# Expert blocks of a decoder layer: gate and up computed with features on partitions, from weights copied by VectorE, with grouped loads and later sums

## The chip, the cores and the metric

The kernel runs on one core of a Trainium2 chip. The metric is the device time of one execution in microseconds (us), less is better; for several executions the median is given. One execution was also taken by the hardware profiler. The profile's engines are TensorE (PE for matmuls, PEld for its weight loads), VectorE (DVE), ScalarE (ACT), GpSimd (POOL) and SyncE (SP); a q behind a name is that engine's sequencer, which handles waits, registers and the issue of DMAs.

## The reference

One decoder layer in fp32 on x of 16 sequences x 256 tokens x 256 features: attention with rope and a Taylor softmax, an additive cross term, and a mixture of experts. Only the last part is touched:

```python
shared = silu(x @ ws_gate) * (x @ ws_up) @ ws_down
scores = sigmoid(x @ gate_w.T)                       # 16 experts
topk_w, topk_idx = top_k(scores, 2)
topk_w = topk_w / (topk_w.sum(-1) + 1e-20) * 2.5
g = einsum('th,ehm->etm', x, w_gate)                 # h 256, m 128
u = einsum('th,ehm->etm', x, w_up)
eo = einsum('etm,emh->eth', silu(g) * u, w_down)
out = einsum('te,eth->th', route, eo) + shared
```

The reference computes all experts for all tokens; the kernel computes for each token only its two chosen ones.

## The kernel before

**First stage.** Attention and the cross term run sequence by sequence, in an order written out by hand (ORDER, DRAIN). At its end each token is normalised, its two experts are chosen, and the row (256 features, the two weights, the expert's code and the destination, 264 numbers in all) is scattered twice by GpSimd's indirect DMA into the DRAM tensor `listed`, in which each expert owns whole blocks of 128 rows. The weights of all experts lie in SBUF: `wgu_sb` for gate and up, `wd_sb` for down.

**Block stage.** There are NB = 79 blocks at most; the last five are run only if they are needed, under a branch (`unusual_blocks`), and were not needed here. The other USUAL = 74 run in a loop of steps (lines 1180 to 1206) whose instruction order on each engine is the order of the code, since the loop is under a manual schedule. A block i passes through:

- load, nine steps ahead (AHEAD): one DMA on SP of 128 rows, line 272, into one of 14 buffers `rows`; the first six go to room in `h3T`, from `begin_blocks`.
- `turn`, step i: two TensorE transposes (line 283) put features on partitions, ScalarE copies them to `rowsT` (line 286).
- `pick`, step i: three VectorE operations on one number per row (lines 293, 296, 300) find the weight of the row and its destination.
- `hidden_product`, step i+2: `gu` with tokens on partitions, the rows stationary and the expert's weights moving (line 308, an address from a register that `expert_of` loads for four blocks at a time, line 350). ScalarE takes Silu of the gate half (line 314).
- `weigh`, step i+2: VectorE multiplies Silu, the row's weight and the up half (line 318).
- `turn_hidden`, step i+3: a TensorE transpose `th` (line 325), VectorE copies it to `hidT` (line 327).
- `give`, step i+4: down (line 331), ScalarE copies it out of PSUM to `got` (line 337), GpSimd scatters the rows to `given` in DRAM (line 338), at the destination.

An fp32 matmul is issued as two MATMUL instructions, each with a weight load of its own, a transpose as one. So a step has four MATMULs of line 308, one of 325, two of 331 and two of 283.

**Sums.** When all blocks that can hold rows of a sequence have been given, SP fetches the two results of its 256 tokens (`fetch`, line 1100), at the step in `due`: three steps (LANDED) after the last give, near the end one. VectorE adds them to `x_all` in four adds of 128x256 (line 1120), one a step, the first FETCHED = 6 steps after the fetch; then SP stores the sequence (line 1114). What is left over at the end of the loop is added in the tail (`tail_adds`), between the shared experts of the last four sequences (`SharedLate`, lines 1134 to 1149), which fill TensorE while the last scatters land.

**Queues and buffers.** SP issues block loads, fetches and stores in program order and waits in that order. VectorE, ScalarE and GpSimd run their instructions in program order. PSUM has two buffers each for `tp`, `gu`, `th` and `eo`. The pools of the block stage reuse memory of the first stage, so that the first instructions there wait for many semaphores.

Of the kernel before, what the change touches and what calls it, by code (L numbers as in the profile page):

```python
# [44 lines left out]
F32 = mybir.dt.float32  # L45
# [31 lines left out]
def decoder_kernel(  # L77
# [188 lines left out]
    codes = None  # L266

    class Block:
        def __init__(self, i, home, rows=None, rowsT=None):
            self.i, self.home, self.rowsT = i, home, rowsT  # L270
            self.rows = self.tile("rows", [P, ROW]) if rows is None else rows
            ins = nc.sync.dma_start(out=self.rows, in_=listed[ts(i, P)])
            behind(ins, enlisted)
            enlisted.clear()
# [13 lines left out]
        def pick(self):  # L288

            code, own = self.rows[:, D + 2 : D + 3], codes[:, self.i : self.i + 1]  # L290
            self.weight = self.tile("weight", [P, 1])
            self.dest = self.tile("dest", [P, 1], I32)
            nc.vector.scalar_tensor_tensor(
                self.weight, code, own, self.rows[:, D : D + 1], ALU.is_equal, ALU.mult
            )
            nc.vector.scalar_tensor_tensor(
                self.dest, code, own, self.rows[:, D + 3 : D + 4], ALU.is_equal, ALU.add
            )

            nc.vector.tensor_tensor(  # L300
                self.weight, self.weight, self.rows[:, D + 1 : D + 2], ALU.max
            )

        def hidden_product(self, e):
            self.e = e
            gu = self.gu = self.tile("gu", [P, 2 * M])
            for k in range(KT):
                nc.tensor.matmul(  # L308
                    gu, lhsT=self.rowsT[:, k],
                    rhs=wgu_sb[:, ds(e, 1), k].rearrange("p a i m -> p (a i m)"),  # L310
                    start=(k == 0), stop=(k == KT - 1),
                )
            self.hid = self.tile("hid", [P, M])
            nc.scalar.activation(self.hid, gu[:, 0:M], AF.Silu)  # L314

        def weigh(self):

            nc.vector.scalar_tensor_tensor(  # L318
                self.hid, self.hid, self.weight, self.gu[:, M : 2 * M],
                ALU.mult, ALU.mult,  # L320
            )
# [765 lines left out]
    with tc.tile_pool(name="ew", bufs=3) as ew, tc.tile_pool(  # L1087
# [92 lines left out]
        for i in range(max(due) + 1):  # L1180
# [4 lines left out]
            if 2 <= i < USUAL + 2:  # L1185
                blocks[i - 2].hidden_product(expert[i - 2])
# [68 lines left out]
```

## Time and profile before

| | us |
|---|---|
| median of five executions | 505.56 (504.3 to 509.84) |
| the profiled execution | 505.42 |
| its span, first to last instruction | 503.6 |
| TensorE busy | 471.6 |
| VectorE busy | 385.8 |
| ScalarE busy | 329.3 |
| GpSimd busy | 321.9 |
| granted TensorE clock, mean | 0.992 |
| block stage, from the first gate-up product to the end | 362.4 to 503.6 |

The span is cut into slices in the page, and for each engine the busy share is given in tenths. A table by windows gives for a stretch the busy time of PE, PEld, DVE, ACT and POOL with the number of their instructions, then the granted clock, the share of the DMA engines and the GB/s. In a timeline a line is start, duration, engine, source line, operation, out<-in, shape and count; merged instructions have the duration of their union. A bracket tells how long the engine stood idle before and what ended that. The duration of a MATMUL includes its drain, which overlaps the next one's stream, so that the cost of one in a sequence is the distance to the next start.

### The profile page before, as it was taken

Reading aid. Unit: us, or ns where it says so; the run is one execution under the profiler, and the core shown is the slowest. Engines: PE = TensorE matmul, PEld = TensorE weight load, DVE = VectorE, ACT = ScalarE, POOL = GpSimd, SP = SyncE. Lnnn points to the kernel's source line nnn. Section 1 sums busy time; section 2 is a strip of 40 time slices with the busy share of each in tenths; the row PEclk is TensorE's granted clock in tenths of the full one; section 3 lists DMA queues with packets and bytes.
Section 4 is the critical chain, followed back from the end, with each engine's and each line's share of the span. In section 5 each row is a group of like instructions: output and inputs, shape, how many; then the busy total and the mean of one; then the engine's idle time right before and its main releaser. Section 6 shows DMA issues by size and latency. Waiting matters only on the chain. (4 is left out here: it accounts for less than half of the span.)

```text
span 503.6 us, 12732 instructions
## 1 busy us (share of the span) xinstructions
PE 471.6 (94%) x4078; PEld 315.4 (63%) x4078; DVE 385.8 (77%) x1607; ACT 329.3 (65%) x783; POOL 321.9 (64%) x539
## 2 busy tenths in 40 slices
PE   2999999999999999999999999988799999999994
PEld 1455656656656656656656655545588888887882
DVE  5745557879989989989989877998555567766766
ACT  2378789887787887887887898331255555555530
POOL 5765346687888888888886666575155665555550
PEclk9999999999999999999999999998999999999998
DMA  7896551342333323321210211111565367987765
GB/s 206 253 342 214 172 171 33 96 131 75 117 77 125 117 73 131 117 79 61 65 44 25 56 33 55 44 54 54 145 211 167 100 203 237 299 286 265 224 196 178
DMA packets 61139, 69.68 MB, mean 138 GB/s; under 512 B 7164, under 2 KB 52493, under 8 KB 61072
## 3 DMA queue, kind: packets, MB, share of 16 engines
q1 hardware_dynamic: 53760, 50.88, 34.0%
q0 software_dynamic: 6624, 17.05, 9.1%
q10 hardware_dynamic: 688, 0.92, 0.6%
q8 instruction: 34, 0.56, 0.5%
q14 instruction: 33, 0.27, 0.2%
HBM read 36.89 MB, written 33.24 MB: 139 GB/s over the span
## 5 line engine op out<-in xcount | busy, mean ns | idle before, releaser
L655 ACT ACTIVATE a<-sc 128x1024 f32<-128x1024 f32 x128 | 124.7, 1032 | 25.1 <-PE sc L645 24.3
L338 POOL DMA_INDIRECT given<-block_got,block_dest x74 | 72.7, 983 | 62.3 <-ACT block_rowsT L286 42.0
L901 POOL DMA_INDIRECT listed<-h,slots x64 | 66.9, 1046 | 16.3 <-issue 15.8
L645 PE MATMUL sc<-qT,kT 32*128 32x256 f32 x1024 | 75.7, 401 | 0.9 <-ACT a L655 0.9
L308 PE MATMUL block_gu<-wgu_sb,block_rowsT 128*128 x288 | 74.4, 381 | 0.1
L645 PEld LDWEIGHTS sc<-qT,kT 32*128 32x128 f32 x1024 | 47.5, 184 | 31.1 <-ACT kT L589 9.1
L665 PE MATMUL av<-a,vaug 128*32 128x256 f32 x1024 | 65.8, 381 | 0.1
L549 PE MATMUL pq<-wqkv,hT 128*128 128x512 f32 x128 | 64.4, 629 | 0.7 <-ACT hT L539 0.7
L327 DVE COPY block_hidT<-block_th 128x128 f32<-128x128 f32 x74 | 21.6, 292 | 40.9 <-PE block_th L325 27.9
L571 POOL TENSOR_TENSOR qkr<-rot,m 128x512 f32<-128x512 f32 x32 | 41.0, 1285 | 17.6 <-DVE m L565 9.5
L308 PEld LDWEIGHTS block_gu<-wgu_sb,block_rowsT 128*128 128x128 f32 x288 | 49.2, 190 | 4.4 <-ACT block_hid L314 0.3
L381 POOL TENSOR_TENSOR rs<-rs,neg_half 128x2 f32<-128x2 f32 x64 | 48.1, 752 | 5.3
L314 ACT ACTIVATE block_hid<-block_gu 128x128 f32<-128x128 f32 x74 | 20.6, 278 | 35.9 <-PE block_gu L308 12.9
L331 PE MATMUL block_eo<-wd_sb,block_hidT 128*128 x148 | 44.1, 381 | 0.0
L665 PEld LDWEIGHTS av<-a,vaug 128*32 128x32 f32 x1024 | 29.3, 110 | 21.2 <-issue 6.3
L387 POOL TENSOR_SCALAR h<-x_all,neg,rs 128x256 f32<-128x256 f32 x64 | 40.1, 632 | 3.4
L337 ACT COPY block_got<-block_eo 128x256 f32<-128x256 f32 x74 | 27.6, 373 | 20.2 <-issue 14.9
L676 ACT ACTIVATE xs<-av,vsum 128x256 f32<-128x256 f32 x64 | 27.3, 485 | 16.4 <-PE av L665 16.4
L559 DVE TENSOR_TENSOR rot<-pq,cosf 128x512 f32<-128x512 f32 x32 | 22.0, 686 | 17.9 <-PE pq L549 17.8
L549 PEld LDWEIGHTS pq<-wqkv,hT 128*128 128x128 f32 x128 | 23.0, 199 | 19.6 <-issue 17.3
L597 PE MATMUL pv<-wqkv,hT 128*128 128x256 f32 x128 | 30.4, 380 | 0.2 <-DVE m L565 0.2
L711 PE MATMUL py<-wo_sb,wvT 128*128 128x256 f32 x128 | 30.4, 380 | 0.0
(190 smaller groups left out, 978.6 us busy)
## 6 DMA issues: line engine op xcount, KB each, us to landing
listed<-empty SPq DMA_DIRECT2D x9, 1056.0 KB
block_rows<-listed SPq DMA_DIRECT2D x68, 132.0 KB
sum<-given SPq DMA_DIRECT2D x15, 512.0 KB
x_all<-in_x_dram SPq DMA_DIRECT2D x16, 256.0 KB
c<-in_ctx_dram SPq DMA_DIRECT2D x16, 256.0 KB
out_dram<-x_all SPq DMA_DIRECT2D x15, 256.0 KB
enc_row<-enc_rows SPq DMA_DIRECT2D x16, 128.0 KB
wgu_sb<-in_L_ffn_w_gate_dram SPq DMA_DIRECT2D x16, 128.0 KB
```

What stands on the lines that cost most here:

```text
L308: nc.tensor.matmul(gu, lhsT=self.rowsT[:, k], rhs=wgu_sb[:, ds(e, 1), k].rearrange("p a i m -> p (a i m)"), start=(k == 0), stop=(k == KT ...
L331: nc.tensor.matmul(eo, lhsT=self.hidT, rhs=wd_sb[:, ds(self.e, 1)].rearrange("m a d -> m (a d)"), start=True, stop=True,)
L338: ins = nc.gpsimd.indirect_dma_start(out=given, out_offset=bass.IndirectOffsetOnAxis(ap=self.dest, axis=0), in_=got, in_offset=None, bound ...
L381: nc.gpsimd.tensor_tensor(r, r, neg_half, ALU.pow)
L387: nc.gpsimd.tensor_scalar(h[:, t, 0:D], src[:, t], neg[:, t : t + 1], r[:, t : t + 1], ALU.add, ALU.mult)
L549: nc.tensor.matmul(pq.rearrange("p h i two -> p (h i two)"), lhsT=self.hT[:, k, ts(t, P)], rhs=wqkv[:, k, 0 : 2 * D], start=(k == 0), stop ...
L571: nc.gpsimd.tensor_tensor(self.qkr[:, t], self.rot[t].rearrange("p h d -> p (h d)"), self.m2[t].rearrange("p h i two -> p (h i two)"), ALU ...
L597: nc.tensor.matmul(self.pv[:, t], lhsT=self.hT[:, k, ts(t, P)], rhs=wqkv[:, k, 2 * D : 3 * D], start=(k == 0), stop=(k == KT - 1),)
L645: nc.tensor.matmul(scs[j // 2][:, j % 2, kt], lhsT=self.kT[rows, g % 2, g // 2, ts(kt, P)], rhs=self.qT[rows, g // 2], start=True, stop=True,)
L655: nc.scalar.activation(a, self.scs[g][i], AF.Square, bias=1.0, scale=HD**-0.5)
L665: nc.tensor.matmul(self.av[ts(j, 32), g % 2], lhsT=self.va[:, kt, head], rhs=self.a[g, j // 2][:, j % 2, kt], start=(kt == 0), stop=(kt == ...
L901: ins = nc.gpsimd.indirect_dma_start(out=listed, out_offset=bass.IndirectOffsetOnAxis(ap=self.slots[:, i, t : t + 1], axis=0), in_=self.h3 ...
```

## The change

- `hidden_product` makes `gu` with features on partitions: the expert's weights are stationary and `rowsT` moves, gate and up for themselves, 128 columns each. The result needs no turn, so `turn_hidden` and its PSUM buffers are gone; `gu` and `eo` have three buffers each.
- The stationary weights come from a tile `w` (four buffers): `weights`, step i, is a VectorE copy of 128x512 from `wgu_sb` at an address from a register. VectorE therefore loads the expert's number too.
- The row's weight is no longer applied in the gating product (`gated`, two operands) but as a scale per partition in the copy of down's result from PSUM on ScalarE.
- A `Group` loads four blocks with one DMA from block 6 on, into one of five buffers, and picks for four blocks at once, in four VectorE operations of 128x4. The first six blocks have a group each, with loads and picks for themselves.
- `give` comes at step i+3, the fetches one step earlier with it, and FETCHED is 9 with five buffers `sum`.

The DMAs that load the blocks are now, in program order on SP, 17 of four blocks and the first six of one. Per block TensorE has eight MATMULs for gate and up in place of four, and two each for down and the turn of the rows as before. VectorE's order in a step is: the copy for block i, the gating of block i-2, in one step of four the picks, then an add. The first instruction of the stage on VectorE is the register load, then the copy for block 0.

```diff
+    class Group:
+        def __init__(self, i, n, home, rows=None):
...
+                self.rows = self.tile("rows", [P, n, ROW])
+            ins = nc.sync.dma_start(
+                out=self.rows, in_=listed[i * P : (i + n) * P].rearrange("(n p) d -> p n d", p=P)
+            )
...
+        def pick(self):
...
+            first, second, code, last = (self.rows[:, :, D + i] for i in range(4))
+            own = codes[:, self.i : self.i + self.n]
...
+            nc.vector.tensor_tensor(same, code, own, ALU.is_equal)
+            nc.vector.tensor_tensor(self.weight, same, first, ALU.mult)
+
+            nc.vector.tensor_tensor(self.weight, self.weight, second, ALU.max)
+            nc.vector.tensor_tensor(self.dest, same, last, ALU.add)
...
-        def hidden_product(self, e):
+        def weights(self, e):
             self.e = e
-            gu = self.gu = self.tile("gu", [P, 2 * M])
-            for k in range(KT):
-                nc.tensor.matmul(
-                    gu, lhsT=self.rowsT[:, k],
-                    rhs=wgu_sb[:, ds(e, 1), k].rearrange("p a i m -> p (a i m)"),
-                    start=(k == 0), stop=(k == KT - 1),
-                )
-            self.hid = self.tile("hid", [P, M])
-            nc.scalar.activation(self.hid, gu[:, 0:M], AF.Silu)
-
-        def weigh(self):
-            nc.vector.scalar_tensor_tensor(
-                self.hid, self.hid, self.weight, self.gu[:, M : 2 * M],
-                ALU.mult, ALU.mult,
-            )
-
-        def turn_hidden(self):
-            th = self.tile("th", [P, M])
-            nc.tensor.transpose(th, self.hid, ident)
-            self.hidT = self.tile("hidT", [M, P])
-            nc.vector.tensor_copy(self.hidT, th)
+            self.w = self.tile("w", [P, KT, 2, M])
+            nc.vector.tensor_copy(self.w.unsqueeze(1), wgu_sb[:, ds(e, 1)])
+
+        def hidden_product(self):
+            gu = self.gu = self.tile("gu", [M, 2, P])
+            for i in range(2):
+                for k in range(KT):
+                    nc.tensor.matmul(
+                        gu[:, i], lhsT=self.w[:, k, i], rhs=self.rowsT[:, k],
+                        start=(k == 0), stop=(k == KT - 1),
+                    )
+            self.hid = self.tile("hid", [M, P])
+            nc.scalar.activation(self.hid, gu[:, 0], AF.Silu)
+
+        def gated(self):
+            nc.vector.tensor_tensor(self.hid, self.hid, self.gu[:, 1], ALU.mult)
...
-                eo, lhsT=self.hidT,
+                eo, lhsT=self.hid,
...
-            nc.scalar.copy(got, eo)
+            nc.scalar.activation(got, eo, AF.Copy, scale=self.weight)
...
-            owner_row[:, i : i + n], engines=(mybir.EngineType.PE,), min_val=0, max_val=E - 1,
+            owner_row[:, i : i + n], min_val=0, max_val=E - 1,
+            engines=(mybir.EngineType.PE, mybir.EngineType.DVE),
...
-            got = ew.tile([P, TT, 2, D], F32, tag="sum", name="sum", bufs=4)
+            got = ew.tile([P, TT, 2, D], F32, tag="sum", name="sum", bufs=5)
...
-        AHEAD, LANDED, FETCHED = 9, 3, 6
+        AHEAD, LANDED, FETCHED = 9, 3, 9
...
-            step = last + 4 + (LANDED if last + 4 < USUAL - AHEAD else 1)
+            step = last + 3 + (LANDED if last + 3 < USUAL - AHEAD else 1)
...
+            if i < USUAL:
+                blocks[i].weights(expert[i])
             if 2 <= i < USUAL + 2:
-                blocks[i - 2].hidden_product(expert[i - 2])
-            if 3 <= i < USUAL + 3:
-                blocks[i - 3].turn_hidden()
+                blocks[i - 2].hidden_product()
             if i == USUAL + 2:
                 late[0].gate_up()
-            if 4 <= i < USUAL + 4:
-                blocks[i - 4].give()
+            if 3 <= i < USUAL + 3:
+                blocks[i - 3].give()
             if 2 <= i < USUAL:
                 blocks[i].turn()
             if 2 <= i < USUAL + 2:
-                blocks[i - 2].weigh()
+                blocks[i - 2].gated()
...
-            if i + AHEAD < USUAL:
-                blocks.append(Block(i + AHEAD, home))
+            load_blocks(i + AHEAD + 1)
```

## The prediction

> **What bounds the kernel now.** I read the page from the top: busy shares, slices, then the chain of waits, then the windows. TensorE is the bound almost throughout, and its granted clock is full.
>
> ```profile
> PE 471.6 (94%) x4078; PEld 315.4 (63%) x4078; DVE 385.8 (77%) x1607; ACT 329.3 (65%) x783; POOL 321.9 (64%) x539
> PE   2999999999999999999999999988799999999994
> PEclk9999999999999999999999999998999999999998
> ```
>
> The change touches only the block stage, about 362 us to the end. The table by windows shows that TensorE has no gap there in 84 us, VectorE is 64% busy and GpSimd 58%:
>
> ```profile
> 366.00:450.00 84.00, 84.00 (x467) 70.98 (x466) 53.61 (x283) 47.81 (x156) 48.96 (x50) 1.00 0.68 213
> ```
>
> So what a step costs is the sum of its matmul passes. The timeline of one step (start, duration; MATMULs overlap their drains, so I take distances between starts):
>
> ```profile
> 402.53 1.03 PE L308 MATMUL block_gu<-wgu_sb,block_rowsT 128*128 x4
> 403.39 0.27 PE L325 MATMUL block_th<-ident,block_hid 128*128 128x128 f32 x1
> 403.50 0.60 PE L331 MATMUL block_eo<-wd_sb,block_hidT 128*128 x2
> 403.94 0.38 PE L283 MATMUL block_tp<-ident,block_rows 128*128 128x128 f32 x2
> 404.16 1.03 PE L308 MATMUL block_gu<-wgu_sb,block_rowsT 128*128 x4
> ```
>
> Gate and up 0.86, turn of hid 0.11, down 0.44, two turns of rows 0.22: 1.63 us (exactly, 1.627: from 366 to 450 every step repeats to 0.01). 74 such steps are the stage.
>
> **Steady step.** Removed on TensorE: block_th, 0.11. Gate and up go from four passes of 256 columns (0.86) to eight of 128. No row has eight such passes in a run, but two come near: a pair of full 128-column fp32 passes, and passes of 32 columns whose pace can only be their weight load.
>
> ```profile
> 353.87 0.38 PE L1012 MATMUL po<-ident,total 128*128 128x128 f32 x2
> 344.77 0.38 PE L796 MATMUL ahead<-both,tri 128*128 128x32 f32 x2 [1.63 <-DVE norm L829]
> 344.99 0.39 PE L796 MATMUL ahead<-both,ones 128*128 128x32 f32 x2
> ```
>
> In the first, one pass takes 0.274 and two together 0.38, so the second starts 0.11 after the first. In the others two passes come each 0.22, so a weight load costs 0.11 too, though its record says 0.19: loads overlap. Eight passes: 8 x 0.110 = 0.88 (0.872 at 0.109, 0.896 at 0.112). The far bound, loads not overlapped at all, 8 x 0.19 = 1.52, is excluded by those rows. New step 0.88 + 0.434 + 0.218 = 1.532, against 1.627: -0.095 (-0.079 to -0.103). Over 70 steps, the first four being counted below: **-6.65** (-5.5 to -7.2).
>
> **What must hide beside it.** VectorE, by distances between starts in the same step: turn copy 0.20, weigh 0.26, three picks 0.33, an add 0.42: 1.21. The turn copy and the picks go (-0.53). Four picks of a whole group come once in four steps (dependent small operations follow each other in 0.21 on lines 877 to 881, so 0.6, 0.15 a step). That leaves 0.83. The weight copy, 128x512 from SBUF to SBUF, has no row. Above: the add of 512 columns at line 949, 0.605 from start to start (0.68 in the record). Below: half of its 0.53 of streaming, 0.34. VectorE is then 1.17 to 1.44 of 1.532: hidden by TensorE at either end, with little to spare at the upper one, so the sum does not turn on it; I take the middle, 0.47, which makes 1.30. A register load on VectorE each four steps (0.54 at line 1026) runs on its sequencer under the add.
>
> The Trainium skill, VectorE: DVE Perf Modes, section "The perf-mode tier table", gives an fp32 SBUF copy twice the rate (1227 ns for 2048), which as an estimate makes 0.42 us of ours and VectorE 1.25 a step, hidden, so the sum stays; no run here shows one. A rule against the change stands in the Trainium skill, SBUF — State Buffer, "Who interferes with whom": a copy in that mode and a GpSimd instruction hold one port pair and exclude each other for a whole instruction. By it VectorE could wait for a DMA_INDIRECT, and the sum would be about that of rival 2 in place of 499.3. The nearest row does not show that: a 16-column TENSOR_SCALAR on SBUF took 0.17 at 346.24, inside a DMA_INDIRECT from 346.19 to 347.17.
>
> ScalarE: the eviction got takes a scale per partition. COPY 0.373 now; a Copy with a scale at line 589 took 0.761 for 512 against 0.592 without, so +0.1 to +0.17: 0.28 + 0.37 + 0.5 = 1.15 a step, hidden. GpSimd: 0.98 a step, unchanged. Dependence: hid must be gated before down. TensorE has down, two turns and the next gate and up between (0.43 + 0.22 + 0.88 = 1.53); Silu 0.28, gating 0.34 and hand-overs take 0.8, so 0.7 is spare for a VectorE that runs late. Behind a late gating the next picks, add and weight copy queue; the copy is two steps early.
>
> Loads: SP issues 17 of 528 KB in place of 68 of 132 KB, same bytes, at least nine steps ahead (13.8 us), with 20 blocks of room against 14: 0. Should one be late, the turn of that block stops TensorE. Sums nine steps behind a fetch, three more than now: waits for them are 1.4 us in all, three times, most of it in the tail: 0 (-0.4). The output stores move back with the adds on SP, the fetches one step forward with give; both wait there for what they do now. A third PSUM buffer for gate-up and down takes the place of the turn's: 0, nothing waits for one now.
>
> **Start.** Here the copy is on the path: TensorE's first product needs it.
>
> ```profile
> 361.62 0.69 DVE L949 TENSOR_TENSOR x_all<-x_all,shared_eo 128x512 f32<-128x512 f32 x1 [0.70 <-PE shared_eo L942]
> 362.40 0.22 DVE L293 SCALAR_TENSOR_TENSOR block_weight<-h3T 128x1 f32<-128x1 f32 x1
> 362.41 1.10 PE L308 MATMUL block_gu<-wgu_sb,h3T 128*128 x4 [0.83 <-DVE x_all L949]
> ```
>
> VectorE's first block operation comes at 362.40 after its waits; now a register load (0.35 to 0.54) goes before them and the copy (0.34 to 0.69) must end: TensorE starts 0.9 to 1.3 later. Then VectorE has copy, four picks (0.6), copy, picks, copy before the first gating, some 2.4 to 3.2 after its start, while TensorE wants it 2.0 after its own: another 0.2 to 0.8. Together **+1.5** (+1.0 to +2.1).
>
> **Tail.** Give follows gating by one step instead of two, and the turn is gone.
>
> ```profile
> 482.40 1.03 PE L308 MATMUL block_gu<-wgu_sb,block_rowsT 128*128 x4
> 484.34 1.89 PE L1134 MATMUL late_ps<-h3T,wgu_sb 128*128 128x256 f32 x8
> 486.07 1.03 PE L331 MATMUL block_eo<-wd_sb,block_hidT 128*128 x4
> 488.62 0.98 POOL L338 DMA_INDIRECT given<-block_got,block_dest  x1 [0.30 <-issue]
> 496.56 3.27 DVE L1120 TENSOR_TENSOR x_all<-x_all,sum 128x256 f32<-128x256 f32 x8 [0.93 <-DMA sum<-given]
> 499.75 0.74 DVE L1149 TENSOR_TENSOR x_all<-x_all,late_eo 128x256 f32<-128x256 f32 x2
> ```
>
> Gate and up of the last block end at 483.26; its scatter starts 5.36 later. Now: down of block 72 0.43, late gate and up 1.73, down 0.43, eviction 0.7, 0.1: 3.4, a gain of 2.0 up to the fetch. But three more adds (3 x 0.39) are left for the tail. VectorE had 0.93 of idle before the last eight adds; it now reaches them about 12.3 after gate and up, with the fetch landed at 11.3, against 13.3 before. **-1.0** (-2.0 to +0.3).
>
> **Sum.** -6.65 + 1.5 - 1.0 = -6.15. The profiled execution took 505.42 (span 503.6 and 1.8 around it), 0.14 under the median of 505.56. 505.42 - 6.15 = **499.3**.
>
> **Rivals.** Let s be the step; the whole is 505.9 + 70 x (s - 1.627).
> 1. VectorE is just late: copy at 0.605, loads and waits of its sequencer not hidden (0.1 to 0.15), s = 1.59: **503.3**. For: picks add 0.45 in one step of four and the register load stands ahead of a copy. Against: 0.7 of slack.
> 2. Slower: the weight copy waits on VectorE for GpSimd. s = 0.83 + c, c the copy with its wait. No gain from c = 0.79; 1% slower (s above 1.695) from c = 0.87. A wait of half a DMA_INDIRECT, 0.49 on 0.47, gives s = 1.79: **517.3**. For: GpSimd is in one for 0.98 of each step. Against: the row at 346.24.
> 3. The change buys nothing because transfers set the pace: s stays 1.627, **505.9**. For: DMA slices at 9 tenths with 299 GB/s about 430. Against: no TensorE wait on rows anywhere from 366 to 450.
> 4. More gain: two pauses at 452 and 462, in which VectorE and ScalarE stood for up to 2.2 us, cost TensorE some 1.6 in all (window 450 to 483: 31.90 of 33.00 busy, and stretched ends). If late sums cause them, nine steps end them, and the tail gives its 2.0: **496.7**.
>
> **How the numbers follow.** Forecast 0.57 (its own range 497.5 to 501.5), rival 1 0.19, rival 2 0.13, rival 3 0.05, rival 4 0.06. Leaving out rival 2 and part of the edges, 496.5 to 506.0 holds about 0.8. A difference under 1% (500.5 to 510.6) is about what a measurement of this kernel cannot tell from none. Faster by more: 0.47 of the forecast's 0.57, all of rival 4 and little of rival 1, 0.55. Slower by more: 0.12 of rival 2. Rest 0.33.
>
> **What would show it.** Gate and up as eight passes 0.11 apart, TensorE full at a distance of 1.53 between blocks; the weight copy at 0.4 to 0.7, VectorE 80 to 90% busy; first product near 363.5; last adds without idle time before them. Wrong if passes come over 0.115 apart, if the copy or the DMA_INDIRECT stretches (rival 2), or if down waits for gating (rival 1).

## The result, and the profile after

| | before | after |
|---|---|---|
| median, us | 507.04 (504.18 to 511.93, 94 executions) | 506.36 (502.73 to 511.75, 52 executions) |
| ratio after / before | | 0.9986, 95% interval 0.9973 to 1.0 |
| profiled execution, us | 505.42 | 508.26 |
| its span, us | 503.6 | 506.4 |
| start of gate and up of block 3 | 366.72 | 372.48 |
| from there to gate and up of block 73 (70 steps) | 115.67 | 113.97 |
| from there to the end | 21.24 | 20.00 |

The forecast was 499.3 (496.5 to 506.0): a gain of 6.15 us, of which 0.7 came, a difference that cannot be told from none. The three rows below the span carry the rest of this text. Their changes, +5.76, -1.70 and -1.24, make the +2.8 by which the two spans differ. The profiled execution of the changed kernel lay 1.9 above its median and that of the kernel before 1.6 below, which leaves the -0.7.

First the page of the changed kernel: busy time, TensorE's slices and its clock.

```profile
PE 468.2 (92%) x4300; PEld 323.3 (64%) x4300; DVE 380.6 (75%) x1477; ACT 335.2 (66%) x783; POOL 325.1 (64%) x539
PE   1899999999999999999999999997699999998994
PEclk9999999999999999999999999999789999999999
```

Two things differ from the page before. The clock dips further, in slices 29 and 30 (about 354 to 380), where the blocks begin, and TensorE is a little less than full towards the end. The table by windows (start:end, length, busy time of PE, PEld, DVE, ACT, POOL with counts, clock, DMA share, GB/s) splits the stage:

```profile
376.00:430.00 54.00, 54.00 (x421) 50.47 (x420) 29.77 (x113) 35.53 (x106) 34.79 (x35) 1.00 0.54 171
430.00:486.00 56.00, 52.45 (x391) 47.52 (x390) 36.14 (x129) 31.77 (x98) 33.82 (x34) 1.00 0.79 253
```

In the first 54 us TensorE has no gap; in the next 56 it has 3.5 us of them. The step itself, from the timeline:

```profile
402.58 0.97 POOL L360 DMA_INDIRECT given<-block_got,block_dest  x1 [0.40 <-ACT block_rowsT L320]
402.74 0.60 PE L353 MATMUL block_eo<-wd_sb,block_hid 128*128 x2
403.18 0.38 PE L317 MATMUL block_tp<-ident,block_rows 128*128 128x128 f32 x2
403.38 0.47 ACT L359 ACTIVATE block_got<-block_eo,block_weight 128x256 f32<-128x256 f32 x1 [0.16 <-PE block_eo L353]
403.40 1.06 PE L340 MATMUL block_gu<-block_rowsT,block_w 128*128 128x128 f32 x8
403.46 0.42 DVE L333 COPY block_w<-wgu_sb 128x512 f32 x1
404.13 0.97 POOL L360 DMA_INDIRECT given<-block_got,block_dest  x1 [0.57 <-ACT block_rowsT L320]
404.29 0.60 PE L353 MATMUL block_eo<-wd_sb,block_hid 128*128 x2
```

Gate and up take 0.89 to the next down (403.40 to 404.29), down 0.44, the two turns 0.22: a step of 1.546. The weight copy takes 0.42, the eviction with its scale 0.47.

One of the gaps behind 430 (2.3 us from block to block):

```profile
432.00 1.20 POOL L360 DMA_INDIRECT given<-block_got,block_dest  x1 [0.30 <-ACT block_got L359]
432.11 0.60 PE L353 MATMUL block_eo<-wd_sb,block_hid 128*128 x2
432.77 1.06 PE L340 MATMUL block_gu<-block_rowsT,block_w 128*128 128x128 f32 x8
433.69 0.28 ACT L345 ACTIVATE block_hid<-block_gu 128x128 f32<-128x128 f32 x1 [1.74 <-PE block_tp L317]
434.00 0.29 DVE L349 TENSOR_TENSOR block_hid<-block_hid,block_gu 128x128 f32<-128x128 f32 x1 [1.30 <-ACT block_hid L345]
434.34 0.70 PE L353 MATMUL block_eo<-wd_sb,block_hid 128*128 x2 [0.51 <-DVE block_hid L349]
```

The gate and up ahead of the down at 432.11 had ended by 432.28, and its Silu starts only at 433.69, 1.41 late, with nothing else on ScalarE. In between TensorE goes through the gate and up of the next block, then waits for the late chain. The semaphore records show the same from the other side: three updates of TensorE that belong to 432.3, 432.7 and 432.9 all come at 433.66 to 433.75. I call a Silu late when it starts more than 0.4 after the end of the last gate and up that had ended by then; this profile has 13 late Silus in 74, all behind 428, that of the kernel before 3.

The start, by the timeline:

```profile
361.34 1.91 PE L965 MATMUL shared_eo<-wd_sb,shared 128*128 128x256 f32 x4
363.30 0.69 DVE L972 TENSOR_TENSOR x_all<-x_all,shared_eo 128x512 f32<-128x512 f32 x1 [3.50 <-PE shared_eo L965]
364.62 0.43 DVE L333 COPY block_w<-wgu_sb 128x512 f32 x1 [0.64 <-DVE x_all L972]
365.26 2.05 PE L340 MATMUL block_gu<-h3T,block_w 128*128 128x128 f32 x8 [2.00 <-issue]
```

And by the windows, whose last but two column is the clock:

```profile
357.70:361.10 3.40, 1.30 (x7) 0.67 (x6) 1.28 (x2) 0.37 (x1) 0.00 (x0) 1.00 0.68 192
361.20:364.50 3.30, 2.06 (x6) 1.16 (x4) 0.69 (x1) 0.37 (x1) 0.00 (x0) 0.50 0.18 43
364.60:367.90 3.30, 2.64 (x12) 2.67 (x13) 2.14 (x12) 0.41 (x2) 0.00 (x0) 0.50 0.96 300
368.00:371.30 3.30, 3.30 (x15) 3.01 (x15) 1.99 (x12) 1.22 (x4) 0.22 (x1) 0.50 1.10 361
371.40:374.80 3.40, 3.40 (x28) 3.20 (x28) 1.93 (x12) 2.03 (x6) 1.96 (x3) 1.00 0.50 168
```

The first product waits for the copy, as foreseen, at 365.26 in place of 362.41. What was not foreseen is the clock column: from 361.15 to 371.39 TensorE runs at half clock, after a stretch in which it was busy for 1.30 of 3.40. The last shared down takes 1.91 in place of 1.03, the first gate and up 2.05 in place of 1.06.

And the tail:

```profile
490.88 1.17 POOL L360 DMA_INDIRECT given<-block_got,block_dest  x1 [1.19 <-ACT block_got L359]
499.59 3.27 DVE L1143 TENSOR_TENSOR x_all<-x_all,sum 128x256 f32<-128x256 f32 x8 [0.27 <-DMA sum<-given]
```

The last scatter starts 4.43 after the start of the last gate and up (486.45) and, counted as the prediction counts, 3.54 after its end (487.34, where the next product starts) in place of 5.36; the forecast said 3.4. The last eight adds have 0.27 of idle time before them in place of 0.93.

### The profile page after: what moved, and what is told of

The parts are those of the page before. It is cut to its first block, busy times and chain, and to the rows that moved or that the text cites. A ratio compares the mean times of both kernels' runs of the same rounds, so it can differ in the third digit from the quotient of the medians.

```text
span 506.4 us, 12865 instructions
## 1 busy us (share of the span) xinstructions
PE 468.2 (92%) x4300; PEld 323.3 (64%) x4300; DVE 380.6 (75%) x1477; ACT 335.2 (66%) x783; POOL 325.1 (64%) x539
## 5 line engine op out<-in xcount | busy, mean ns | idle before, releaser
L360 POOL DMA_INDIRECT given<-block_got,block_dest x74 | 75.9, 1026 | 61.2 <-ACT block_rowsT L320 32.3
L340 PE MATMUL block_gu<-block_rowsT,block_w 128*128 128x128 f32 x576 | 76.8, 276 | 0.7 <-ACT block_got L359 0.5
L340 PEld LDWEIGHTS block_gu<-block_rowsT,block_w 128*128 128x128 f32 x576 | 70.6, 193 | 1.2 <-ACT block_got L359 0.7
L349 DVE TENSOR_TENSOR block_hid<-block_hid,block_gu 128x128 f32<-128x128 f32 x74 | 21.2, 287 | 45.8 <-ACT block_hid L345 39.1
L353 PE MATMUL block_eo<-wd_sb,block_hid 128*128 x148 | 45.5, 389 | 2.9 <-DVE block_hid L349 1.9
L359 ACT ACTIVATE block_got<-block_eo,block_weight 128x256 f32<-128x256 f32 x74 | 35.1, 474 | 12.5 <-PE block_eo L353 7.0
L333 DVE COPY block_w<-wgu_sb 128x512 f32 x74 | 32.7, 442 | 2.9 <-issue 2.3
```

Source lines behind the costliest of these rows:

```text
L340: nc.tensor.matmul(gu[:, i], lhsT=self.w[:, k, i], rhs=self.rowsT[:, k], start=(k == 0), stop=(k == KT - 1),)
L353: nc.tensor.matmul(eo, lhsT=self.hid, rhs=wd_sb[:, ds(self.e, 1)].rearrange("m a d -> m (a d)"), start=True, stop=True,)
L359: nc.scalar.activation(got, eo, AF.Copy, scale=self.weight)
L360: ins = nc.gpsimd.indirect_dma_start(out=given, out_offset=bass.IndirectOffsetOnAxis(ap=self.dest, axis=0), in_=got, in_offset=None, bound ...
```

## The experiments

The theories at the outset. A: the start costs 4 us more than forecast, by the wait for the first copy and the clock. B: late semaphores stop ScalarE and VectorE, and with down only one step behind, TensorE stands. C: chance. The kernels of one session ran on one chip, here called chip A or chip B, beside the kernel before; the rows stand by sessions: again to both, before2 to single, before8 to bsums, after3 to relief, then relief2 and plain. The chip of the first comparison is not known. Columns: ratio to before with its interval; start of block 3; the 70 steps from block 3 to 73; the undisturbed step; late Silus before and after 428 us.

| run | chip | median | ratio | block 3 | 70 steps | step | late |
|---|---|---|---|---|---|---|---|
| before, first profile | | 507.04 | | 366.72 | 115.67 | 1.627 | 0, 3 |
| after, first profile | | 506.36 | 0.9986 (0.9973 to 1.0) | 372.48 | 113.97 | 1.546 | 0, 13 |
| again (after) | A | 511.53 | 1.0107 (1.0069 to 1.0144) | 369.60 | 120.35 | 1.546 | 18, 17 |
| early | A | 510.93 | 1.0081 (1.005 to 1.0113) | 366.98 | 119.07 | 1.546 | 13, 18 |
| give4 | A | 512.91 | 1.011 (1.0054 to 1.0165) | 369.41 | 119.56 | 1.546 | 18, 16 |
| both | A | 510.57 | 1.006 (1.0031 to 1.009) | 366.31 | 119.43 | 1.546 | 15, 18 |
| before2 (before) | A | 509.17, one | | 369.45 | 116.38 | 1.628 | 0, 3 |
| after2 (after) | A | 513.11 | 1.0111 (1.0078 to 1.0144) | 371.40 | 119.79 | 1.546 | 11, 21 |
| nocopy | A | 508.03 | 1.0027 (1.0001 to 1.0053) | 370.79 | 117.75 | 1.546 | 6, 22 |
| single | A | 515.00 | 1.0164 (1.0122 to 1.0207) | 372.46 | 123.51 | 1.546 | 19, 19 |
| before8 | B | 511.98 | 1.0092 (1.0061 to 1.0122) | 369.47 | 118.93 | 1.655 | 0, 7 |
| after4 | B | 560.77 | 1.1068 (1.1022 to 1.1114) | 370.55 | 166.32 | 2.379 | 0, 0 |
| bgroup | B | 508.54 | 1.0023 (0.9996 to 1.005) | 369.58 | 117.28 | 1.628 | 0, 2 |
| bsums | B | 509.18 | 1.0032 (1.0003 to 1.006) | 370.17 | 116.27 | 1.628 | 0, 3 |
| after3 (after) | B | 514.38 | 1.0117 (1.0081 to 1.0153) | 372.91 | 121.39 | 1.546 | 17, 19 |
| eight2 (= before8) | B | 510.91 | 1.0053 (1.003 to 1.0076) | 367.08 | 118.97 | 1.655 | 0, 8 |
| four | B | 507.65 | 0.9988 (0.9954 to 1.0022) | 369.92 | 115.93 | 1.516 | 8, 12 |
| relief | B | 507.47 | 0.9985 (0.9963 to 1.0007) | 369.00 | 117.13 | 1.629 | 0, 1 |
| relief2 | B | 510.65 | 1.0059 (1.003 to 1.0087) | 370.06 | 119.59 | 1.546 | 10, 16 |
| plain | B | 500.54 | 0.986 (0.9825 to 0.9896) | 367.85 | 107.99 | 1.546 | 0, 0 |

### The change again, and again

again, after2 and after3 are the changed kernel as it is, in three sessions.

> The changed kernel once more, unchanged. Theory A (start: TensorE's wait for the first weight copy, and the half clock that comes of it, cost 4 us more than forecast): a half-clock record of at least 6.8 us lies between 355 and 375 again, and gate and up of block 3 starts after 370. Theory B (pauses: from about 430 on ScalarE and VectorE stand for 1 to 2 us several times, and with down only one step behind gate and up TensorE waits for them): blocks 3 to 73 take 112 to 115 us, against 108.2 for 70 undisturbed steps of 1.546. Rival C (chance: the profiled execution fell on a bad clock, the edit has nothing to do with it): half clock falls elsewhere, block 3 starts by 368.5. Time: 505 to 508 by all.

> The changed kernel once more, as the control of this call. 506 to 512, with 13 to 35 Silus more than 0.4 us late, and blocks 3 to 73 in 113 to 121 us; whether near the lower or the upper end tells how far it differs from chip to chip. Theories H and C both expect late Silus here.

> The changed kernel as the control of this call: 506 to 513 us, 13 late Silus (over 0.4 us) with none in the first half on a chip like that of the first profile, 31 to 35 on a chip like that of the repeated runs.

On both chips the changed kernel is 1.1% slower than before, where the first comparison says equal. The kernel before takes what it always took (506.8 to 508.4 in the sessions). The profiles differ from the first one in the late Silus: 32 to 36 in place of 13, from 381 to 391 us on in place of 434, and 70 steps in 120 to 121 us. So the lateness varies between chips, or between loads of the program, for this kernel and hardly for the one before. The half clock at the start was there each time, 3.41, twice 3.41, and 10.24 us long. again misses the signs of both theories all the same: A wanted 6.8 of half clock and block 3 after 370 (3.41 and 369.60), B 112 to 115 for the 70 steps (120.35).

### The start

early: the copies of blocks 0 and 1 and their register load go ahead of the last shared add, into columns of `h3T` that are free by then.

```diff
+        def first_weights():
+            first_experts.extend(expert_of(0, 4))
+            for i in range(2):
+                room = h3T[:, :, ds(first_free[5] * TB * P + 2 * i * M, 2 * M)]
+                blocks[i].weights(first_experts[i], room.rearrange("p k (a m) -> p k a m", a=2))
...
-                        steps_over += [(99, begin_blocks), (2, unusual_blocks), (1, first_turns)]
+                        steps_over += [(99, begin_blocks), (2, unusual_blocks), (1, first_turns), (0, first_weights)]
```

> The weight copies of blocks 0 and 1, with their register load, go ahead of the last shared add, into columns of h3T that are free by then; all else as in the changed kernel. Theory A: gate and up of block 3 starts 3 to 5 us earlier than in the changed kernel (by 368), no half-clock record past 366, and the time falls by 2.5 to 4.5 us. Rival C: the clock falls as before, block 3 comes 0.9 to 1.3 earlier at most, time within 1.3 us. Theory B expects nothing of this edit in blocks 3 to 73 (112 to 115 us).

Timeline of early, where the copies now lie under the wait for the rows of block 0:

```profile
359.69 0.76 DVE L333 COPY h3T<-wgu_sb 128x512 f32 x2
361.87 0.69 DVE L972 TENSOR_TENSOR x_all<-x_all,shared_eo 128x512 f32<-128x512 f32 x1 [1.42 <-PE shared_eo L965]
362.70 1.13 PE L340 MATMUL block_gu<-h3T 128*128 128x128 f32 x8 [0.87 <-DVE x_all L972]
```

The first product waits for the shared add alone, as in the kernel before, and block 3 comes at 366.98, 2.6 to 5.9 earlier than in the three profiles of the control, with no half clock before 504. So far theory A. But the time falls by 0.6 against again, its control, as 31 late Silus stay; both, the same edit on give4, has no half clock there either and is 2.3 below give4. The start is thus worth less than the 2.5 to 4.5 that A expected.

### Down one step later

give4: `give` at i-4, as in the kernel before, with a fourth buffer for `hid`; both: early and give4.

```diff
-            if 3 <= i < USUAL + 3:
-                blocks[i - 3].give()
+            if 4 <= i < USUAL + 4:
+                blocks[i - 4].give()
```

> Down, eviction and scatter go four steps behind the fetch of a block in place of three, with a fourth buffer for the hidden rows; the sums' due steps move with them by one. Theory B: the pauses of ScalarE and VectorE are still in the trace, but TensorE stands still for them far less: blocks 3 to 73 take 108.5 to 110.5 us in place of 114.0; the tail grows by 0.5 to 1.5; time 1.5 to 4 us less. Rival (the pauses hit TensorE's own queue, or the steady step itself is long): blocks 3 to 73 take 112 to 115 still, time the same or up to 1.5 more. Theory A: the start as in the changed kernel, block 3 after 370.

> The two edits together (early copies for blocks 0 and 1, down one step later). If A and B are both right and independent: block 3 by 368, blocks 3 to 73 in 108.5 to 110.5, time 4 to 8 us below the changed kernel, some 499 to 502 (the forecast was 499.3). If only A is right: 2.5 to 4.5 less; if only B: 1.5 to 4 less; if neither, within 1.3.

Theory B fails in its remedy. With a whole step more of slack the 70 steps take 119.6, close to the 120.35 of the control; 26 of 70 steps are at 1.546, 21 at 1.62 to 1.67, where ScalarE runs a step behind and TensorE waits for its `rowsT`, and 18 are longer. One reading, not shown, is that a late chain is not absorbed when the next late Silu comes two or three steps later (387.5, 392.0, 395.9, 400.4).

### Copies, loads, and the kernel before on the same chip

before2 is the kernel before, for a profile of it on chip A. nocopy takes expert 0's weights where they lie; single issues the rows of each block as its own load.

```diff
-            self.w = self.tile("w", [P, KT, 2, M])
-            nc.vector.tensor_copy(self.w.unsqueeze(1), wgu_sb[:, ds(e, 1)])
+            self.w = wgu_sb[:, 0]
```

```diff
+        def load(self, j):
+            ins = nc.sync.dma_start(out=self.rows[:, j], in_=listed[ts(self.i + j, P)])
```

> The kernel before, unchanged, profiled on the chip of the other runs of this call. In the repeated runs ScalarE's Silu came 0.8 to 1.6 us after gate and up had ended in every third or fourth step, since semaphores came late. If that belongs to the chip (theory H), this trace shows it too, 15 to 35 Silus more than 0.4 us late, and TensorE's blocks 3 to 73 still take 114 to 117 us, since its slack hides them. If it belongs to the change (theory C), it shows 0 to 5 late Silus, as the first profile of the kernel before did (3), and 114 to 116 us.

> No weight copies and no register load on VectorE: gate and up take the weights of expert 0 for every block straight from where they lie (left out: the choice of the expert in gate and up). Theory V (the 0.42 us copies on VectorE, beside GpSimd's scatters, make the pauses): late Silus fall to 0 to 5, scatters go from 1.03 back to 0.98, blocks 3 to 73 take 108 to 110 us, and with the start 3 us earlier the time falls by 8 to 12 against the control. Rival S (pauses come of late semaphores whatever VectorE does; ScalarE's 1.15 of 1.55 leaves too little to catch up): late Silus as many as in the control, blocks 3 to 73 within 2 us of it, time 2 to 4 less, from the start alone.

> Rows loaded block by block again (132 KB each, nine steps ahead), all else as changed; picks still by four. Theory L (528 KB loads bunch the transfers and delay semaphores): late Silus fall to 0 to 8, blocks 3 to 73 take 108.5 to 111, time 3 to 8 below the control. Rivals V and S: no difference from the control beyond 1.5 us, late Silus as many.

The lateness belongs to the change and not to the chip alone: before2 has 3 late Silus, after2 32. VectorE's copies alone are not its cause: nocopy has 28. They are not free either: nocopy is 5.1 us faster than after2 beside it, between the 2 to 4 that rival S expected and the 8 to 12 of theory V. Of the 3.5 by which the two spans differ, 0.6 lie before block 3, 2.0 in the 70 steps and 0.8 behind; which property of the copies costs the 2.0 is not shown. What they do to the scatters is small. The group of the scatters in after3 (count, busy, mean ns, idle before them):

```profile
L360 POOL DMA_INDIRECT given<-block_got,block_dest x58 | 59.9, 1033 | 40.6 <-ACT block_rowsT L320 26.9 <-issue 8.0 <-DVE block_w L333 3.4
```

And in nocopy:

```profile
L359 POOL DMA_INDIRECT given<-block_got,block_dest x59 | 57.8, 980 | 41.3 <-ACT block_rowsT L320 32.9 <-issue 6.1 <-ACT block_got L358 0.8
```

Beside copies a scatter is 0.05 longer. A copy that lies wholly inside a scatter need not be longer, as the first profile shows; others there took up to 0.65:

```profile
413.40 0.97 POOL L360 DMA_INDIRECT given<-block_got,block_dest  x1 [0.57 <-ACT block_rowsT L320]
413.43 0.43 DVE L333 COPY block_w<-wgu_sb 128x512 f32 x1
```

Loads by four are no cause either: single is worse, by 1.9 us than after2 beside it and by 3.5 than again of another session, with 38 late Silus.

### Fewer and more passes; the other parts of the change alone

before8 (and eight2, the same kernel on the same chip B beside a control) gives the kernel before eight passes of 128 columns; after4 and four give the changed kernel 256 columns in each.

```diff
-                nc.tensor.matmul(
-                    gu, lhsT=self.rowsT[:, k],
-                    rhs=wgu_sb[:, ds(e, 1), k].rearrange("p a i m -> p (a i m)"),
...
+            for i in range(2):
+                for k in range(KT):
+                    nc.tensor.matmul(
+                        gu[:, ts(i, M)], lhsT=self.rowsT[:, k],
+                        rhs=wgu_sb[:, ds(e, 1), k, i].rearrange("p a m -> p (a m)"),
```

```diff
-                        gu[:, i], lhsT=self.w[:, k, i], rhs=self.rowsT[:, k],
+                        gu[:, i], lhsT=self.w[:, k, i], rhs=self.rowsT,
```

(after4; four drops the loop over k as well and takes k = 0.) bgroup and bsums are the kernel before with the change's loads and picks, and with its `FETCHED = 9` and five buffers.

> The kernel before, with gate and up of each block in eight TensorE passes of 128 columns in place of four of 256 (gate columns, then up columns): nothing else moves. TensorE's steady step stays near 1.64 (8 x 0.112 for 4 x 0.215), but it goes through 26 matmul and weight-load instructions a step in place of 18. Theory N (semaphores come late where TensorE goes through more than some number of instructions in a time): 15 to 35 Silus more than 0.4 us late, as in the changed kernel on this chip, against 5 in the kernel before; time 1 to 8 us above the kernel before, the less the more its slack of two steps hides. Rival E (the layout with features on partitions, its shorter chain and fuller ScalarE make the lateness): at most 6 late Silus, time within 2.5 us of before.

> The changed kernel, with gate and up of each block in four TensorE passes of 256 columns: each weight piece meets both halves of the turned rows at once (so the sum over the halves is left out, and gate and up are not the reference's); Silu and gating read as many columns as now. TensorE goes through 16 matmul and weight-load instructions a step in place of 24, in a steady step of 1.51 to 1.53. Theory N: late Silus fall from 31 to 0 to 6, blocks 3 to 73 take 106 to 109 us in place of 118 to 120, time 8 to 12 us below the changed kernel on the same chip, some 500 to 504. Rival E: as many late Silus, blocks 3 to 73 at 114 to 119, time at most 3 less.

> The kernel before with the change's loads and picks alone: rows of four blocks in one load of 528 KB, picks by four. In the changed kernel the loads by four were worth 1.5 to 2.5 us against single loads. If that carries over, time 0.5 to 2.5 below the kernel before; if it is only worth something where ScalarE has no spare, within 0.7 of it. The first steps could lose 0.3 to 0.8 by the larger first loads.

> The kernel before with the change's sums alone: added nine steps behind a fetch in place of six, five buffers in place of four. The forecast gave this 0 in the loop (-0.4 at most) and three more adds of 0.39 in the tail: within 1.2 us of before, more likely above it. If the pauses at 452 to 464 come of sums that wait for their fetch, they go, and the time falls by 1.5 to 3.

> The kernel before with gate and up in eight passes of 128 columns (26 TensorE instructions a step in place of 18), again, beside a control. Its first run stood on another chip and had 7 late Silus and 58 us of blocks 3 to 38, that is no pauses there. Theory N (number of TensorE instructions): at least half as many late Silus as the control. Rival E (the changed kernel's chain and ScalarE): at most 8 late Silus, whatever the control has.

> The changed kernel with gate and up in four TensorE passes of 256 columns in place of eight of 128: only the first half of the contraction is taken, against both halves of the turned rows (so gate and up are not the reference's). 16 TensorE instructions a step in place of 24, at a steady step of 1.51 to 1.53. Theory N: at most 5 late Silus, blocks 3 to 73 in 106 to 109 us, time 4 to 12 below the control. Rival E: late Silus within a third of the control's, time within 3 of it.

The number of TensorE instructions is not what makes the lateness. eight2 has 26 a step and 8 late Silus, after3 beside it 24 a step and 36, four 16 a step and still 20. For the times it is less clear: four is 6.7 below after3, inside the 4 to 12 of theory N, where the shorter step explains 2.1 (70 x 0.030); before8 and eight2 are 4.2 and 2.5 above the kernel before, where the longer step explains 1.9. What the rest is was not looked for. after4 missed its aim: each matmul is two MATMULs, so its four are eight passes, the step is 2.379 and the instructions a step are as many as before. It is of use all the same: at that pace the changed kernel has no late Silu at all. Neither of the other parts pays in the kernel before: loads by four +0.2% (-0.04 to +0.5), sums nine steps behind +0.3% (0.03 to 0.6), and a step of 3.03 at 457 stays.

### ScalarE, or what every block needs once

relief is nocopy with VectorE evicting the turned rows; relief2 puts that copy behind the gating.

```diff
-            nc.scalar.copy(self.rowsT, tp)
+            if 2 <= self.i < USUAL:
+                nc.vector.tensor_copy(self.rowsT, tp)
+            else:
+                nc.scalar.copy(self.rowsT, tp)
```

> The changed kernel without weight copies (weights of expert 0 for all blocks; the expert's choice in gate and up is left out), and VectorE in ScalarE's place evicts the turned rows: ScalarE 0.76 of a step of 1.546, VectorE 1.3. Theory S (ScalarE, 1.15 of 1.546, has too little to catch up after a late semaphore): late first Silus remain, but the half-microsecond ones behind them go, and blocks 3 to 73 take 3 us less than the 116 of the same kernel with ScalarE evicting them. Rival (the lateness itself passes to TensorE): within 1.5 us of 116, on a chip with as many late semaphores.

> As relief (no weight copies, weights of expert 0 for all blocks, VectorE evicts the turned rows), but VectorE does so behind the gating instead of ahead of it, so that down need not wait: steady step 1.546 in place of 1.629. Theory S (ScalarE's 1.15 of a step makes or lets in the lateness): 0 to 6 late Silus at a step of 1.546, blocks 3 to 73 in 108.5 to 112, time 3 to 6 below relief's. Theory G (something that every block needs once, at 1.6 us or so, is overrun by a step of 1.546): 20 to 36 late Silus again, blocks 3 to 73 in 114 to 120, time above relief's.

In plain SyncE stores the rows of a block in order, and GpSimd does nothing in the stage:

```diff
-            ins = nc.gpsimd.indirect_dma_start(
-                out=given,
...
+            ins = nc.sync.dma_start(out=given[ts(self.i, P)], in_=got)
```

> The changed kernel, with SyncE storing each block's rows in order into a larger buffer in place of GpSimd's scatter (the placing of the rows by token is left out, so the sums add other rows): the same bytes, nothing on GpSimd. Theory G, if the thing is GpSimd's scatter: at most 6 late Silus at a step of 1.546, blocks 3 to 73 in 108.5 to 112, time 5 to 10 below the changed kernel on this chip. Theory S, or G with another thing than the scatter: late Silus as in the changed kernel, 20 to 36, time within 3 us of it. SyncE's queue has 74 more issues of 0.4 to 0.5, which could hold up loads: TensorE's waits for rows would show that.

relief looked like the answer, with 1 late Silu beside a control with 36, but its step had become 1.629, for down waits for the gating there. relief2, with the same light ScalarE at 1.546, has 26 late Silus. So ScalarE's load is not it. plain decides. Windows of six kernels, all on chip B, columns as above; first after3:

```profile
376.00:426.00 50.00, 47.77 (x358) 43.29 (x356) 23.98 (x93) 28.28 (x88) 29.33 (x30) 1.00 0.42 144
426.00:476.00 50.00, 46.11 (x336) 41.17 (x336) 31.15 (x113) 26.76 (x85) 29.77 (x28) 1.00 0.78 256
```

The same windows of relief:

```profile
376.00:426.00 50.00, 50.00 (x372) 46.71 (x370) 24.86 (x97) 22.98 (x61) 29.32 (x31) 1.00 0.52 168
426.00:476.00 50.00, 48.82 (x357) 45.02 (x357) 33.35 (x120) 22.21 (x60) 29.18 (x30) 1.00 0.80 262
```

Of relief2:

```profile
376.00:426.00 50.00, 47.87 (x360) 43.72 (x359) 25.50 (x93) 20.71 (x60) 29.23 (x31) 1.00 0.50 167
426.00:476.00 50.00, 46.67 (x344) 42.10 (x344) 31.34 (x112) 19.52 (x56) 29.48 (x29) 1.00 0.77 247
```

Of four:

```profile
376.00:426.00 50.00, 48.30 (x249) 40.62 (x250) 26.64 (x100) 30.69 (x92) 30.49 (x32) 1.00 0.53 171
426.00:476.00 50.00, 46.75 (x238) 38.14 (x237) 33.00 (x117) 28.61 (x89) 29.40 (x30) 1.00 0.81 258
```

Of eight2:

```profile
376.00:426.00 50.00, 50.00 (x395) 46.99 (x394) 29.39 (x159) 27.72 (x90) 29.63 (x31) 1.00 0.55 179
426.00:476.00 50.00, 49.18 (x374) 44.89 (x373) 35.00 (x173) 25.86 (x87) 28.88 (x29) 1.00 0.78 257
```

And of plain:

```profile
376.00:426.00 50.00, 50.00 (x391) 46.79 (x390) 27.61 (x106) 32.76 (x98) 0.00 (x0) 1.00 0.74 221
426.00:476.00 50.00, 50.00 (x389) 46.74 (x389) 34.71 (x128) 32.87 (x97) 0.00 (x0) 1.00 0.93 291
```

With GpSimd's column at zero TensorE has no gap in 100 us, at the fast step and at the highest DMA share of all. ScalarE's longest waits from 376 to 476 in after3 (us in total, times, longest):

```profile
ACT block_hid L345 <- PE block_tp L317: 13.9, 11, 1.6
ACT block_hid L345 <- PE block_gu L340: 12.8, 19, 2.0
```

And the longest of plain:

```profile
ACT block_hid L345 <- PE block_gu L340: 24.1, 65, 0.4
```

In plain all 65 waits are the ordinary 0.4; not one Silu is late, the 70 steps take 107.99 (70 x 1.546 = 108.2), and the time is 500.54.

The POOL counts of the other five are 28 to 32 in each 50 us, whether the step is 1.516, 1.546, 1.629 or 1.655. That is one scatter a block, so the count repeats the pace of the stage and does not say what sets it. What is shown is this: with the scatter the 70 steps came out at 1.63 to 1.76 a block in all profiles but that of after4, however short the undisturbed step, which is where the kernel before already was (115.67 / 70 = 1.65); without it plain's came at 1.54. The kernels with an undisturbed step of 1.628 or more have 0 to 8 late Silus, those with a shorter one and the scatter 20 to 38 on these chips.

It is not a fixed pace that the scatter cannot exceed. In the first profile 35 scatters went out at 1.546 between 376 and 430 while TensorE had no gap, and relief, whose step is longer, is through its 70 steps in 117.13, before relief2 (119.59) and after3 (121.39). On that chip the shorter step beside the scatter was disturbed, and came out slower than the longer one that was not.

What stays open. plain takes away GpSimd's instruction, its queue of packets and the placing of rows together, and which of them disturbs the stage is not told apart. The records do not show a limit: DMA_INDIRECT takes 0.98 to 1.03 in the mean, starts again 0.30 after the last at the earliest, and GpSimd is busy 60%. In the first profile the packets of a scatter end within 0.8 us of it from 376 to 408; behind that its queue stands for up to 4.6 us at a time, but in the kernel before it stands for up to 3.3 between 405 and 450 with no Silu late, so that alone does not make one late. Nor is it shown how a scatter delays semaphores of other engines, or why the first profile has none late before 430. The Trainium skill, NOTIFIC — the notification-queue block, section "Overflow: three behaviours, one of which stalls the engine", describes one way in which engines can be held, a full queue of records; no run here tells whether it acts. No version tried beats both kernels and computes the same; one that scatters less often was not tried.

## Why the prediction was wrong, point by point

- **The bound.** "What a step costs is the sum of its matmul passes" was true of the kernel before, but for 1.8 us of pauses. The step that failed is the one sentence "GpSimd: 0.98 a step, unchanged", which counts the scatter as hidden by its busy time and puts what it does to a shorter step at nothing. The runs showed in its place that the step of 1.546 holds through the stage only without the scatter: 107.99 for the 70 steps in plain against 113.97 in the first profile, which is 6.0 us, and 12 to 13 in the repeated runs of the changed kernel. How the scatter does it stays open.
- **Steady step**, -6.65: the mechanism was right. Passes came 0.112 apart, the upper of the two ends, so 1.546 in place of 1.532. Without the scatter the 70 steps fell by 7.68, from 115.67, as the 1.8 us of pauses in the kernel before went too.
- **VectorE and ScalarE beside it.** The copy took 0.42 in undisturbed steps (0.47 taken), the eviction 0.474 (+0.10, the lower end). Both were hidden, as plain shows. The Trainium skill, VectorE: DVE Perf Modes, section "The perf-mode tier table", led to an estimate of 0.42, and the trace agrees. The rule against the change, in SBUF — State Buffer, "Who interferes with whom", does not show as whole instructions that exclude each other: the copy at 413.43 ran in 0.43 wholly inside a scatter, and others beside one took up to 0.65. The scatters are 0.05 longer for the copies, and nocopy shows that most of the lateness is not from there. The Trainium skill, DMA: Bandwidth & Descriptors, section "SWDGE vs HWDGE vs iDMA", says that transfers issued by SyncE are free of that interference; plain's gain cannot be put down to the copies' interference, since nocopy, with no copies, kept 28 late Silus.
- **Start**, +1.5: +1.13 in plain, where no half clock fell into it (first product at 363.57, the forecast said 363.5), and +5.76 in the first profile. What was left out is the clock, at half for 10.24 us from 361.15 on; with it the start is 4.3 above its forecast, the second miss in that profile beside the 5.0 that the steps fell short. Over the profiles the changed kernel has block 3 at 371.6 in the mean of four, the kernel before (two profiles) and its variants before8, eight2, bgroup and bsums at 368.7 in the mean of six: +2.9. Four of these six show half clock there too (3.41 to 6.83 us), so the clock is a draw that both have. That the longer wait makes it worse is suggested by the +2.9 and by early and both, whose starts have no half clock, but one profile each does not show it.
- **Tail**, -1.0: -1.24 in the first profile, -1.05 in plain; the scatter came 1.8 earlier after the last gate and up, where 2.0 were counted.
- **Loads and sums at 0**: true within 0.6% in the kernel before (bgroup, bsums). In the changed kernel loads by four are worth 1.9 to 3.5.
- **Rivals.** 1, VectorE just late: no, plain. 2, the copy waits for GpSimd: the right engine, since the loss goes with GpSimd's scatter, but by luck, for the copy took 0.42 in undisturbed steps and nocopy, with no copies, has 28 late Silus. 3, transfers set the pace: not by their bytes, plain moves the same at 1.546. 4, the sums' lag ends the pauses: no, bsums keeps them.
- **The sum** holds where what it assumed of the scatter is made true: plain gained 7.6 in span (+1.13 - 7.68 - 1.05) and 6.2 in the medians, where 6.15 were forecast.

## What to carry to other kernels

Before a shorter step is counted, ask what else happens once in every step and how far below the old step it is known to stay; busy time below the step does not show that it can go faster. Take that thing away in one run, early: removing other suspects one by one only moved the question. And when an engine waits for something that has long ended, the dependence that the profile names need not be the cause; here give4, which loosened it, gained nothing, and taking an instruction of another engine away did.

## What the runs showed of the hardware

- Semaphore updates can come late in a bunch, in a stage with a GpSimd scatter every 1.5 us: three of TensorE's, due at 432.28, 432.71 and 432.93, came at 433.66, 433.70 and 433.75 in the first profile. TensorE went on meanwhile with what it need not wait for (the gate and up at 432.77).
- Half clock comes in stretches of 3.41 us and their multiples (3.41, 6.83, 10.24). In the first profile it began after a stretch with 1.30 of 3.40 us busy and ended after the first one without a gap. Over 51 executions of the changed kernel the time falls by 436 us for 1.00 of mean clock, so a stretch (0.5 x 3.41 / 504 = 0.0034) goes with 1.5 us, as an estimate; most of the spread between executions goes with it (correlation r = -0.79). The Trainium skill, TensorE: Matmul & The Clock Gate, section "Part 1: The HAM clock gate (the "warmup" mystery)", gives a free-running window of 3413 ns and calls the outcome variable from run to run; both agree.
- One kernel was level with another in one comparison (0.9986) and 1.1% slower in three others on two chips, while the kernel it is compared with stayed within 506.8 to 508.4.
